# Counting with one input: VectorE's threshold counts as a tensor_scalar with an accumulator, and the memory keys transposed after the tenth folding turn

## The chip, the cores and the metric

The kernel runs on one core of a Trainium2 chip. The core has TensorE (PE; weight loads are shown as PEld), VectorE (DVE), ScalarE (ACT), GpSimd (POOL) and SyncE (SP), which issues the DMAs. The metric is the time of one launch on the device, in microseconds (us); lower is better. Three runs before the change took 2820.49, 2822.4 and 2825.87 us; the median is 2822.4.

## The reference

The input x is 8 batches of 512 tokens of 256 numbers, in fp32. Two layers follow. The first adds to x an attention and an FFN, both of the layer-normed x; the second adds a long convolution with a gated FFN, and an int4 linear layer with a low-rank side branch. The attention is what the change touches (cut to what matters):

```python
# H = 16 heads of DH = 64, NUM_MEM = 64 learned memory keys in front, TOPK = 64
q, k, v = split(x @ Wq.T), split(x @ Wk.T), split(x @ Wv.T)
k, v = concat([mem_k, k]), concat([mem_v, v])
dots = einsum('bhid,bhjd->bhij', q, k) * DH ** -0.5
dots = einsum('bhij,hk->bkij', dots, pre_proj)          # mixes the heads
dots = where(causal, -max, dots)
kth = top_k(dots, TOPK)[0][..., -1:]                     # the 64th largest of each row
dots = where(dots < kth, -max, dots)
attn = einsum('bhij,hk->bkij', softmax(dots), post_proj) # mixes the heads again
out = (attn @ v) @ Wout.T + bout
```

The FFN of the first layer quantises activations and weights to FP4 in blocks of 16 numbers; the int4 layer rounds its weight matrix with one scale for the whole matrix.

## The kernel before

**Stages.** A preparation (0 to about 120 us) loads and transposes weights, quantises the FFN's weights, rounds the int4 matrix and folds Wq, Wk and pre_proj into one matrix per mixed head (`mg`, and `mgm` for the memory keys). Then comes the attention (to about 2200 us), then the rest of both layers (to the end). Beside the attention's last groups, the FFN of batch 0 already runs.

**The folding.** It goes in `NJ` = 20 turns `j`, each over 16 dimensions: turns 0 to 15 over those of x, turns 16 to 19 over the 64 memory keys. A turn multiplies `bd` (block-diagonal copies of Wk, and of the transposed memory keys for the last four turns) with `wq` into a bank `pa`, copies it to `both` (ScalarE in even turns, VectorE in odd ones), multiplies with `kr` (pre_proj spread out) into a bank `pm`, which ScalarE copies to `mg` or `mgm` and squares; VectorE adds the squares up (`sqp`). The sums give, for each mixed head, the size of its scores, from which `first_guesses` computes a first threshold for every row. The memory keys `mk` need eight transposes on TensorE and two copies on VectorE into `bd`; before the change these stand ahead of the first turn in the program.

**The attention.** Queries are taken in 64 groups (8 batches of 8 groups) of 64 tokens; a group has 8 blocks of 8 tokens. One block's scores lie with 16 heads x 8 tokens on the 128 partitions and the keys along the free axis: 64 memory keys and the causal keys, from 72 to 576 numbers in fp32. The 64th largest score of each of the 128 rows is found by counting. `search` makes six rounds (`ROUNDS`); in each, every block counts how many of its scores reach the current threshold `cur`. `na` says how many of a group's 8 blocks ScalarE counts: 8 in the first three rounds, 0 in the last three, which VectorE counts; the first two groups (`EDGE`) and the last four (`LAST`) split some rounds with `na` = 4. ScalarE counts with Sign and an accumulator (L1079), VectorE with a compare and an accumulator (L1083). Both give `raw`; `base[na] - raw` is twice the distance of the count from its aim, whichever engine counted: the table `base` holds one number per block for each `na`. Between rounds `narrow` (L1099 to L1132) makes a secant step to the next threshold: on POOL after ScalarE's rounds, on VectorE after its own. After the sixth round the distance goes to `foff` (L1209).

Then VectorE takes the eight scores just under or over the threshold (`under`, L1140, and MAX8, L1143) and picks the 64th (`pick`, L1148 to L1152); ScalarE computes the exponentials `e` (L1158); VectorE drops what lies below the 64th and sums up (`keep_top`, L1167), and takes the reciprocal `rden` (L1252). POOL multiplies it into the second head mix (`mixd`, L1260), with which TensorE turns the scores (`ps_at`, L1303) and multiplies by the values (`ps_y`, L1327). Ahead of a group, TensorE makes the mixed queries (`ps_mi`, L997) and the scores (`ps_sc`, L1037), which ScalarE copies out (`tk`, L1008, and `ring`, L1043).

**The order.** A planner (`Plan`) with a fixed cost for each operation and due times writes the order of every engine's queue ahead of time. The preparation goes through `Straight`, which records each call, derives dependencies from the tiles that it reads and writes (as ranges of partitions and columns, so two interleaved patterns in one tile count as overlapping), and orders by the longest chain behind an operation; `r.late` shifts an operation's due time. DMAs are planned with the rest and issued by SP in that order. Records made through `Straight` all carry the line L235, so their tiles tell them apart. The pools of the attention take the memory of the preparation, so that the attention's first gather (`rows`, L955) waits for the preparation's last store.

The lines that a sentence can't say are VectorE's count and the two places where it is used:

```python
nc.vector.scalar_tensor_tensor(
    junk, src, thr, two.to_broadcast([P, src.shape[-1]]), ALU.is_ge,
    ALU.mult, accum_out=raw[:, b : b + 1],
)
...
eng.tensor_tensor(cur[:, 1], base[na][:, own], w["raw"], ALU.subtract)
nc.vector.tensor_tensor(w["off"], base[na][:, g * GB : (g + 1) * GB], w["raw"], ALU.subtract)
```

`two` is one column of -2.0 per partition, read again for every key as the second input, so `raw` is -2 times the count.

Of the kernel before, what the change touches and what calls it, by code (L numbers as in the profile page):

```python
# [11 lines left out]
ALU = mybir.AluOpType  # L12
# [7 lines left out]
H, DH = 16, 64  # L20
HC = H * DH // P
MEM = 64
# [4 lines left out]
GB = 8  # L27
# [15 lines left out]
AIM = LOW + 3.5  # L43
# [553 lines left out]
def block_kernel(ctx: ExitStack, tc: tile.TileContext, a: dict, out: bass.AP):  # L597
    nc = tc.nc
# [47 lines left out]
    with ExitStack() as c0:  # L646
# [14 lines left out]

        io8 = keep.tile([P, 8], F32, name="io8")
        base = {}
        for na in sorted({na for na, _ in ROUNDS + EDGE + LAST}):
            base[na] = keep.tile([P, NB], F32, name=f"base{na}")
        minus = keep.tile([P, GB], F32, name="minus")
        good = keep.tile([P, NB], F32, name="good")
# [9 lines left out]
        with tc.tile_pool(name="prep", bufs=1) as prep, tc.tile_pool(name="prep_ps", bufs=1, space=PSUM) as pps:  # L677
# [5 lines left out]
            def bank(kind):  # L683
                own = {"a": banks[:2], "m": banks[2:5], "t": banks[5:]}[kind]
                used[kind] = used.get(kind, -1) + 1
                return own[used[kind] % len(own)]
# [34 lines left out]
            for j0 in range(0, 16, 8):  # L721
                for t in range(2):
                    for i in range(2):
# [3 lines left out]
                            bd[rows, half, j0 : j0 + 8, t, :],  # L727
                            wkm[rows, half, j0 * 16 : (j0 + 8) * 16].rearrange("p c (j i) -> p c j i", i=16),
                        )
            r.late = 30.0  # L730
            ps = bank("t")
            for c in range(HC):
                r.tensor.transpose(
                    ps[:, c * MEM : (c + 1) * MEM],
                    mk[:, 2 * c : 2 * c + 2, :].rearrange("m h d -> m (h d)"),
                    ident[:MEM, :MEM],
                )
            for t in range(2):
                rows = slice(t * DH, (t + 1) * DH)
                r.vector.tensor_copy(bd[rows, :, 16:, t, :], ps[rows].rearrange("p (c j i) -> p c j i", c=HC, i=16))  # L740
            r.late = 0.0

            row16 = prep.tile([P, 16], F32, name="row16")
            r.vector.tensor_reduce(row16, ident.rearrange("p (k i) -> p i k", i=16), AX.X, ALU.add)
# [9 lines left out]
            for j in range(NJ):  # L754
                pa = bank("a")
                for i in range(2):
                    for u in range(4):
                        c = 4 * i + u
                        r.tensor.matmul(
                            pa[u * 32 : (u + 1) * 32, i * D : (i + 1) * D], bd[:, c, j].rearrange("p t i -> p (t i)"),  # L760
                            wq[:, c, :], start=True, stop=True,
                        )
                ab = both[j % 3]
                (r.scalar.copy, r.vector.tensor_copy)[j % 2](ab, pa)
                pm = bank("m")
                for e in range(DC):
                    for i in range(2):
                        r.tensor.matmul(
                            pm[:, e * D : (e + 1) * D], ab[:, i * D + e * P : i * D + (e + 1) * P],
                            kr[:, i].rearrange("p k i -> p (k i)"), start=(i == 0), stop=(i == 1),  # L770
                        )
                dst = mg[:, :, :, j * 16 : (j + 1) * 16] if j < 16 else mgm[:, :, :, (j - 16) * 16 : (j - 15) * 16]
                r.scalar.copy(dst, pm.rearrange("p (e k i) -> p e k i", e=DC, i=16))
                r.scalar.activation(junk[j % 2], pm, AF.Square)
                r.vector.tensor_reduce(sqp[:, j], junk[j % 2].rearrange("p (q i) -> p q i", i=16), AX.X, ALU.add)
# [293 lines left out]
        def block(s, g, b):  # L1069
            return s[:, b, : keys(g * GB + b)]  # L1070

        def count(g, s, cur, raw, b, on_act):


            src = block(s, g, b)
            thr = cur[:, 0, b : b + 1]
            junk = wp.tile([P, WD[-1]], I8, name=f"junk{int(on_act)}")[:, : src.shape[-1]]
            if on_act:
                nc.scalar.activation(  # L1079
                    junk, src, AF.Sign, bias=thr, scale=-1.0, accum_out=raw[:, b : b + 1]  # L1080
                )
            else:
                nc.vector.scalar_tensor_tensor(  # L1083
                    junk, src, thr, two.to_broadcast([P, src.shape[-1]]), ALU.is_ge,
                    ALU.mult, accum_out=raw[:, b : b + 1],
                )

        def narrow(g, w, k, na, on_pool):

# [6 lines left out]
                return st.tile([P] + shape, F32, name=name, bufs=4)  # L1096

            cur, prev = w["cur"], w.get("prev")
            eng.tensor_tensor(cur[:, 1], base[na][:, own], w["raw"], ALU.subtract)  # L1099
            w["prev"] = cur  # L1100
            w["cur"] = nxt = st.tile([P, 2, GB], F32, name="cur", bufs=14)
            by = new("by", [GB])
# [78 lines left out]
        def search(pl, g, s, w, deps, rounds):  # L1181
# [6 lines left out]
            for k, (na, on_pool) in enumerate(rounds):  # L1188
# [4 lines left out]
                tail = pl.add("none", 0.0, open_, [tail])  # L1193
                for b in range(GB):
                    def one_count(b=b, na=na):
                        count(g, s, w["cur"], w["raw"], b, b < na)

                    n = keys(g * GB + b)
                    counts.append(
                        pl.add("ACT", 0.28 + 0.00083 * n, one_count, deps + [tail]) if b < na else  # L1200
                        pl.add("DVE", 0.17 + 0.00105 * n, one_count, deps + [tail])
                    )

                def step(k=k, na=na, on_pool=on_pool):
                    if k < len(ROUNDS) - 1:
                        narrow(g, w, k, na, on_pool)
                    else:
                        w["off"] = st.tile([P, GB], F32, name="foff", bufs=4)
                        nc.vector.tensor_tensor(w["off"], base[na][:, g * GB : (g + 1) * GB], w["raw"], ALU.subtract)  # L1209

                last = k == len(ROUNDS) - 1
                tail = pl.add(
# [659 lines left out]
```

## Time and profile before

| | |
|---|---|
| runs | 2820.49, 2822.4, 2825.87 us (median 2822.4) |
| the profiled execution | 2827.49 us, span 2825.8 us, granted clock 0.951 |
| busy in the span | PE 2531.3, PEld 1963.4, DVE 2440.1, ACT 2031.5, POOL 1191.1 us |
| VectorE's counts, L1083 | 1512 instructions, 578 ns in the mean, and 1512 reads of the accumulator, 81 ns |
| ScalarE's counts, L1079 | 1560 instructions, 562 ns in the mean, and 1560 reads of the accumulator, 196 ns |

A profile is one execution on the chip. A line of a group reads: source line, engine, operation, output tile <- input tiles, shapes, how many; then the busy time and the mean of one in ns; then how long the engine was idle just before them and what ended most of that idle time. In a timeline the first two numbers are the start and the duration in us; "x8" at the end says that eight instructions in a row were merged, and brackets give the idle time before and what ended it. The unit called PEq, POOLq or SPq is the sequencer of that engine.

### The profile page before, as it was taken

What the parts mean: (1) busy time and instruction counts of PE and PEld (TensorE: products, weight loads), DVE (VectorE), ACT (ScalarE), POOL (GpSimd) and SP (SyncE); (2) the same over time, 40 slices, a digit from 0 to 9 for tenths busy, and PEclk for the clock granted to TensorE, in tenths of its full rate; (3) what the DMA queues carried; (4) which work ended last, traced back from release to release, by engine and by line L of the source; (5) the groups of instructions that cost most, each with busy time, mean ns of one, the idle gap of its engine ahead of it and who ended that gap; (6) DMA issues with size and microseconds to landing.
All of it is one profiled execution on the core that took longest, in us unless ns stands there. A gap on an engine that the chain in (4) does not pass through costs nothing. (4 is left out here: it accounts for less than half of the span.)

```text
span 2825.8 us, 57533 instructions
## 1 busy us (share of the span) xinstructions
PE 2531.3 (90%) x19064; PEld 1963.4 (69%) x19064; DVE 2440.1 (86%) x7978; ACT 2031.5 (72%) x5876; POOL 1191.1 (42%) x2215
## 2 busy tenths in 40 slices
PE   5999999999999999999999999999976578999997
PEld 3676877787687778777776786777665455666664
DVE  6678989999999999999999999999989869877762
ACT  3478887888888888888888887887888445544442
POOL 3204544445443544444354444445345344444320
PEclk9999999999999999999999999999988789999998
DMA  4300010100000000001000010000010031000000
GB/s 135 147 26 16 25 30 17 28 19 19 21 26 19 26 21 26 21 19 28 19 27 10 28 30 15 21 21 28 25 42 7 6 109 30 23 16 15 8 8 15
DMA packets 114872, 82.71 MB, mean 29 GB/s; under 512 B 79339, under 2 KB 108806, under 8 KB 113798
## 3 DMA queue, kind: packets, MB, share of 16 engines
q1 hardware_dynamic: 114566, 78.95, 9.2%
q8 instruction: 153, 2.51, 0.4%
q14 instruction: 153, 1.25, 0.1%
HBM read 44.04 MB, written 35.39 MB: 28 GB/s over the span
## 5 line engine op out<-in xcount | busy, mean ns | idle before, releaser
L1079 ACT ACTIVATE junk<-ring,cur 128x312 int8<-128x312 f32 (+26 forms) x1560 | 864.9, 562 | 22.9 <-POOL cur L1185 13.6
L1083 DVE SCALAR_TENSOR_TENSOR junk<-ring,cur,two 128x72 int8<-128x72 f32 (+9 forms) x1512 | 826.9, 578 | 10.4 <-POOL cur L1132 7.8
L1037 PE MATMUL ps_sc<-xnT,tk 128*128 128x8 f32 (+38 forms) x2048 | 540.6, 411 | 52.0 <-ACT ring L1043 51.3
L997 PE MATMUL ps_mi<-rows,mg 128*128 128x128 f32 x4096 | 518.2, 283 | 39.1 <-ACT scr L974 22.5
L997 PEld LDWEIGHTS ps_mi<-rows,mg 128*128 128x128 f32 x4096 | 495.1, 197 | 66.5 <-ACT scr L974 27.8
L1037 PEld LDWEIGHTS ps_sc<-xnT,tk 128*128 128x128 f32 x2048 | 351.6, 201 | 204.7 <-issue 76.1
L1303 PE MATMUL ps_at<-mixd,ring 128*128 128x128 f32 x2560 | 338.9, 284 | 24.1 <-POOL mixd L1260 21.9
L1099 POOL TENSOR_TENSOR cur<-base,raw 128x8 f32<-128x8 f32 x186 | 55.9, 300 | 704.4 <-ACT junk L1079 656.6
L1303 PEld LDWEIGHTS ps_at<-mixd,ring 128*128 128x128 f32 x2560 | 311.8, 195 | 49.8 <-POOL mixd L1260 28.2
L1167 DVE SCALAR_TENSOR_TENSOR ring<-ring,kth,e 128x520 f32<-128x520 f32 (+56 forms) x512 | 276.5, 562 | 75.3 <-ACT e L1158 72.2
L1079 ACT ACTIVATION_READ_ACCUMULATOR junk<-ring,cur 128x1 f32 x1560 | 305.4, 196 | 0.0
L1140 DVE SCALAR_TENSOR_TENSOR y<-ring,cur 128x520 f32<-128x520 f32 (+56 forms) x512 | 295.5, 577 | 3.4
L1143 DVE MAX8 top<-y 128x8 f32<-128x520 f32 (+56 forms) x512 | 255.4, 499 | 17.6
L1043 ACT COPY ring<-ps_sc 128x456 f32<-128x456 f32 (+56 forms) x512 | 186.7, 377 | 112.4 <-PE ps_sc L1037 107.9
L1309 ACT COPY at<-ps_at 128x512 f32<-128x512 f32 x320 | 185.7, 581 | 107.7 <-PE ps_at L1303 105.6
L1327 PE MATMUL ps_y<-at,v 128*64 128x64 f32 (+1 forms) x6144 | 221.5, 225 | 18.7 <-ACT at L1291 12.0
L1158 ACT ACTIVATE e<-ring 128x520 f32<-128x520 f32 (+56 forms) x512 | 229.1, 471 | 12.1 <-DVE ring L1167 11.5
L1327 PEld LDWEIGHTS ps_y<-at,v 128*64 128x64 f32 (+1 forms) x6144 | 197.4, 138 | 55.9 <-ACT at L1291 19.6
L1122 POOL TENSOR_TENSOR by<-gap,minus 128x8 f32<-128x8 f32 x124 | 219.6, 1771 | 9.7
L1008 ACT COPY tk<-ps_mi 128x256 f32<-128x256 f32 x512 | 170.9, 378 | 65.3 <-PE ps_mi L997 64.9
L1260 POOL TENSOR_TENSOR mixd<-mix,rden 128x512 f32<-128x512 f32 x128 | 145.1, 1152 | 141.3 <-DVE rden L1252 95.1
L235 PE MATMUL ps_gu<-mg,ring 128*128 128x352 f32 x448 | 148.4, 476 | 16.5 <-DVE hid L235 10.3
(319 smaller groups left out, 4030.1 us busy)
## 6 DMA issues: line engine op xcount, KB each, us to landing
msd<-scr SPq DMA_DIRECT2D x32, 512.0 KB
ring<-msd SPq DMA_DIRECT2D x512, 32.0 KB
scr<-in_L_attn_x_dram SPq DMA_DIRECT2D x10, 512.0 KB
mg_d<-mg SPq DMA_DIRECT2D x1, 4096.0 KB
att<-o SPq DMA_DIRECT2D x64, 64.0 KB
ring<-in_L_attn_x_dram SPq DMA_DIRECT2D x8, 512.0 KB
ring<-att SPq DMA_DIRECT2D x8, 512.0 KB
out_dram<-ring SPq DMA_DIRECT2D x8, 512.0 KB
```

What stands on the lines that cost most here:

```text
L997: nc.tensor.matmul(ps[:, j * P : (j + 1) * P], mg[:, e, k + j, e2 * P : (e2 + 1) * P], toks(e), start=(e == 0), stop=(e == DC - 1),)
L1037: nc.tensor.matmul(ps[:, :ntok], q["tk"][side_of(g)][e][:, b].rearrange("p k i -> p (k i)"), o["xnT"][:, e, :ntok], start=(e == 0), stop=( ...
L1043: nc.scalar.copy(s[:, b, MEM : MEM + ntok], q.pop(("ps", b))[:, :ntok])
L1079: nc.scalar.activation(junk, src, AF.Sign, bias=thr, scale=-1.0, accum_out=raw[:, b : b + 1])
L1083: nc.vector.scalar_tensor_tensor(junk, src, thr, two.to_broadcast([P, src.shape[-1]]), ALU.is_ge, ALU.mult, accum_out=raw[:, b : b + 1],)
L1122: eng.tensor_tensor(by, gap[:, 1], minus, ALU.pow)
L1140: nc.vector.scalar_tensor_tensor(y, src, cur[:, 0, b : b + 1], src, ALU.is_ge, ALU.subtract, reverse1=True)
L1143: nc.vector.max(out=top[:, b, :], in_=y)
L1158: nc.scalar.activation(e, src, AF.Exp, scale=1.0 / SMALL)
L1167: nc.vector.scalar_tensor_tensor(src, src, kth[:, b : b + 1], e, ALU.is_ge, ALU.mult, accum_out=den[:, b : b + 1])
L1303: nc.tensor.matmul(pt[:n, b * P : (b + 1) * P], s[:, 4 * j + b, col : col + n], w["mix"][j][:, b, :], start=True, stop=True,)
L1327: nc.tensor.matmul(w["py"][j * DH : (j + 1) * DH, q * GR : (q + 1) * GR], vs[c][:n, k * DH : (k + 1) * DH], ats[c][:n, k, :], start=(c == ...
```

## The change

Two things change.

First, where VectorE counts all 8 blocks of a round (`na` = 0), the count becomes a `tensor_scalar`: it compares the scores with the threshold, adds 0.0, and its accumulator adds the result up. It has one input tensor; the column `two` is not read. `raw` is then the count itself, and a new function `excess` turns it into twice the distance from the aim with a multiply and an add, in place of the subtraction from `base`. The table for `na` = 0 goes. Rounds with `na` = 4 or 8 stay as they are.

Second, the transposes and copies of the memory keys move from ahead of the folding turns into turn 9, behind its copy to `both`. In the planner, the last of the transposes also gets that copy as something to come after. The due time's shift of 30 goes.

```diff
-        for na in sorted({na for na, _ in ROUNDS + EDGE + LAST}):
+        for na in sorted({na for na, _ in ROUNDS + EDGE + LAST} - {0}):
...
-            r.late = 30.0
-            ps = bank("t")
-            for c in range(HC):
-                r.tensor.transpose(
-                    ps[:, c * MEM : (c + 1) * MEM],
-                    mk[:, 2 * c : 2 * c + 2, :].rearrange("m h d -> m (h d)"),
-                    ident[:MEM, :MEM],
-                )
-            for t in range(2):
-                rows = slice(t * DH, (t + 1) * DH)
-                r.vector.tensor_copy(bd[rows, :, 16:, t, :], ps[rows].rearrange("p (c j i) -> p c j i", c=HC, i=16))
-            r.late = 0.0
...
-                (r.scalar.copy, r.vector.tensor_copy)[j % 2](ab, pa)
+                op = (r.scalar.copy, r.vector.tensor_copy)[j % 2](ab, pa)
+                if j == 9:
+
+                    ps = bank("t")
+                    for c in range(HC):
+                        mk_op = r.tensor.transpose(
+                            ps[:, c * MEM : (c + 1) * MEM],
+                            mk[:, 2 * c : 2 * c + 2, :].rearrange("m h d -> m (h d)"),
+                            ident[:MEM, :MEM],
+                        )
+                    mk_op.after.append(op)
+                    for t in range(2):
+                        rows = slice(t * DH, (t + 1) * DH)
+                        r.vector.tensor_copy(
+                            bd[rows, :, 16:, t, :], ps[rows].rearrange("p (c j i) -> p c j i", c=HC, i=16)
+                        )
...
-        def count(g, s, cur, raw, b, on_act):
+        def count(g, s, cur, raw, b, na):
+            on_act = b < na
...
+            elif na == 0:
+                nc.vector.tensor_scalar(junk, src, thr, 0.0, ALU.is_ge, ALU.add, accum_out=raw[:, b : b + 1])
             else:
                 nc.vector.scalar_tensor_tensor(
...
+        def excess(eng, to, g, raw, na):
+
+            if na == 0:
+                eng.tensor_scalar(to, raw, 2.0, -2.0 * AIM, ALU.mult, ALU.add)
+            else:
+                eng.tensor_tensor(to, base[na][:, g * GB : (g + 1) * GB], raw, ALU.subtract)
...
-            eng.tensor_tensor(cur[:, 1], base[na][:, own], w["raw"], ALU.subtract)
+            excess(eng, cur[:, 1], g, w["raw"], na)
...
-                        count(g, s, w["cur"], w["raw"], b, b < na)
+                        count(g, s, w["cur"], w["raw"], b, na)
...
-                        nc.vector.tensor_tensor(w["off"], base[na][:, g * GB : (g + 1) * GB], w["raw"], ALU.subtract)
+                        excess(nc.vector, w["off"], g, w["raw"], na)
```

## The prediction

> **What bounds the kernel now.** I read the page first (engines, costliest groups), then the busy time by stretch, then which waits end the idle time of TensorE and VectorE in the middle of the run, then the timelines of single counts, of the start and of the three engines around 1017 us. The page:
>
> ```profile
> PE 2531.3 (90%) x19064; PEld 1963.4 (69%) x19064; DVE 2440.1 (86%) x7978; ACT 2031.5 (72%) x5876; POOL 1191.1 (42%) x2215
> ...
> L1079 ACT ACTIVATE junk<-ring,cur 128x312 int8<-128x312 f32 (+26 forms) x1560 | 864.9, 562 | 22.9 <-POOL cur L1185 13.6
> L1083 DVE SCALAR_TENSOR_TENSOR junk<-ring,cur,two 128x72 int8<-128x72 f32 (+9 forms) x1512 | 826.9, 578 | 10.4 <-POOL cur L1132 7.8
> ```
>
> The line that changes, L1083, is a third of VectorE's time. The stretches show that the 2060 us of attention (140 to 2200) decide:
>
> ```profile
> 0.00:140.00 140.00, 102.58 (x735) 72.70 (x736) 93.92 (x235) 58.45 (x121) 42.96 (x156) 0.96 0.42 142
> 140.00:2200.00 2060.00, 1901.38 (x16163) 1538.12 (x16161) 1896.38 (x6896) 1700.58 (x5274) 909.27 (x1907) 0.96 0.08 23
> ```
>
> The columns are stretch, then PE, PEld, DVE, ACT, POOL busy, clock, DMA share, GB/s. PE is idle for 158.6 us and DVE for 163.6 us there: two engines nearly full, in queues of a fixed order. What ends PE's idle time (300 to 2000 us):
>
> ```profile
> L1037 PE MATMUL ps_sc<-xnT,tk 128*128 128x264 f32 (+61 forms) x1728 | 450.7, 407 | 40.1 <-ACT ring L1043 39.5
> L997 PE MATMUL ps_mi<-rows,mg 128*128 128x128 f32 x3440 | 439.1, 284 | 37.2 <-ACT scr L974 22.5 <-ACT tk L1008 14.7
> L1303 PE MATMUL ps_at<-mixd,ring 128*128 128x128 f32 x2140 | 280.4, 283 | 14.3 <-POOL mixd L1260 13.8 <-ACT at L1309 0.5
> ```
>
> PE waits mostly for ScalarE's evictions, and only 13.8 us for mixd, the one wait behind which VectorE stands (POOL's mixd waits for DVE's rden, 67.1 us in the waits of that window). VectorE's own wait is for ScalarE's exponentials:
>
> ```profile
> L1083 DVE SCALAR_TENSOR_TENSOR junk<-ring,cur,two 128x192 int8<-128x192 f32 (+57 forms) x1287 | 698.7, 573 | 7.3 <-POOL cur L1132 5.3
> ...
> L1167 DVE SCALAR_TENSOR_TENSOR ring<-ring,kth,e 128x200 f32<-128x200 f32 (+61 forms) x431 | 229.3, 554 | 62.0 <-ACT e L1158 59.1
> ```
>
> So VectorE is full, but a microsecond saved on it is not a microsecond of the end.
>
> **The counts.** 1440 of the 1512 counts (all with na = 0) become a tensor_scalar with an accumulator; 72 stay. On all engines the order of the attention's instructions is the same before and after, so only durations change. One count, alone and beside POOL's mixd (first VectorE, then POOL):
>
> ```profile
> 1016.24 0.65 DVE L1083 SCALAR_TENSOR_TENSOR junk<-ring,cur,two 128x416 int8<-128x416 f32 x1
> 1016.81 0.09 DVE L1083 DVE_READ_ACCUMULATOR junk<-ring,cur,two 128x1 f32 x1
> ...
> 1017.46 1.45 DVE L1083 SCALAR_TENSOR_TENSOR junk<-ring,cur,two 128x432 int8<-128x432 f32 x1
> ...
> 1018.83 1.44 DVE L1083 SCALAR_TENSOR_TENSOR junk<-ring,cur,two 128x440 int8<-128x440 f32 x1
> ```
>
> ```profile
> 1017.21 2.59 POOL L1260 TENSOR_TENSOR mixd<-mix,rden 128x512 f32<-128x512 f32 x2 [3.44 <-PE ps_at L1283]
> ```
>
> Undisturbed, the forms 128x408 (634 ns) and 128x416 (641 ns) give n/0.96 + 208 ns. The blocks run from 72 to 576 keys, 324 in the mean, so an undisturbed mean count is 338 + 208 = 546 ns. The page has 578: 32 ns, times 1440 46 us, is time in which a count stands still while POOL reads. The trace has no tensor_scalar with an accumulator. Its neighbours: L302, a tensor_scalar with pointer scalars, 128x256, steps in 1.38/4 = 345 ns = 133 + 212 where two elements pass per cycle; the 128x512 tensor_scalar of the start takes 0.41 us against 0.68 for the two-input form; the accumulator's read (81 ns) stays. Bounds for 1440 counts: half of n/0.96 goes, 169 ns each, 243 us of VectorE less; or one more fixed part, the 65 ns by which pointer forms (208) exceed immediate ones (143), 94 us more. I take one element per cycle and the same fixed part, the nearest rows being the same compare with an accumulator, and the 46 us gone: VectorE's other one-input instruction of this stage, MAX8, takes 0.24 us at 1252.50 beside a mixd as without one, where the two-input L1140 just before it (128x72; a 128x88 alone takes 0.30) took 1.08.
>
> [...]
>
> What of the 46 us reaches the end? The attention's waits that POOL or VectorE end on the other engines, 300 to 2000 us: PE for mixd 13.8, ACT's counts for cur 13.6 + 2.1, VectorE's for cur 5.3, together 35 us; 2060/1700 of that is 42. POOL's short steps are stretched too (L1099 0.64 us at 1001.17 beside a count of 1001.14, its 8-element steps at 1013 us 0.20), so these waits shrink from both sides; on the other hand the next two-input instruction (L1140, L1167) may meet the mixd that a count met. I take 40% of them, 16 us, for the attention, bounds 0 (ScalarE's evictions own the path) and 46 (all of it).
>
> **The excess.** 180 TENSOR_TENSORs (116 at L1099, 64 at L1209, 164 to 219 ns) become tensor_scalars on the same engine in the same place; a short tensor_scalar takes 170 ns (L288, 126.67 us). Between -9 and +5 us of VectorE, none of the end; the waits behind it are those above.
>
> **The memory keys.** Eight transposes and two copies move from the head of PE's and VectorE's queues behind the tenth of twenty folding turns, and the planner, with another longest chain, reorders the start: on SP, Wk, Wq and the two pre_proj loads go ahead of the four w_gate/w_up loads, x, Wv, mk and Wout; VectorE's bd and kr copies ahead of the first weights' quantisation; on PE the first ten turns ahead of the transposes of x, Wv and Wout. Before:
>
> ```profile
> 16.28 1.08 PE L235 MATMUL pps<-ident,mk 64*128 64x64 f32 x8 [16.28 <-DMA mk<-in_L_attn_mem_k_dram]
> ...
> 36.96 3.22 PE L235 MATMUL pps<-ring,bd 128*32 128x256 f32 x32
> ...
> 116.12 0.43 PE L235 MATMUL pps<-sq,ones 128*128 128x64 f32 x2 [0.37 <-DVE sq L235]
> ```
>
> ```profile
> 121.48 0.40 POOL L955 COPY rows<-xnT 128x256 f32<-128x256 f32 x1 [11.65 <-DMA w_d<-w1s]
> ```
>
> Attention starts at 121.48, after the store of w1s. PE's preparation is 83 us of products (73 after 36.96, 10 before). Wk and Wq, 2 MB at the 250 to 370 GB/s of the first 15 us, with bd and kr, let the first turn start near 11 us. Fed without a stop PE would end at 94, 22 us earlier. It isn't: x's transposes wait for VectorE's x rows, which stand behind the second w_gate/w_up pair, issued some 3 us later than before (five small loads now precede it; it landed at 29.8 and 32.6), a stop near 33 to 38 us. The int4 kernel's load overwrites Wv, whose transposes now follow eight turns (to about 45), so its maximum comes near 49 instead of 38.14, and POOL's all-reduce, which held POOL until 49.89, 11 us behind that maximum, holds it to about 60. The second pair's last products thus come 8 to 10 us later, the third pair and w_down follow, each bound to the one before by its two buffers; before, w_down's last steps (102 to 105 us on POOL) waited for PE, not for their loads (VectorE idle until 94.6). I carry 103 for them and some 9 us of products behind: 112 instead of 116.5. That is -4 us, bounds -22 and +10. All engines wait for the store, so it moves the end one for one.
>
> **Sum.** -16 -4 = -20 us on the profiled execution's 2827.5 (span 2825.8 and 1.7 around it), which lies 5.1 over the median of 2822.4; so 2802 for the median. Bounds: -46 -22 and 0 +10. 0.2% (5.6 us) is what a measurement can tell from nothing.
>
> **Rivals.**
> 1. Two elements per cycle. For: the plain form's 0.41 us. Against: no accumulating row shows it. VectorE drops from 1896 to about 1653 us of 2060, no mixd wait is left, and ScalarE's counts and evictions (1701 busy, 77 us of PE's idle time) own the path: 42 us of waits all gone, with the start's 4: about 2776. [...]
> 2. Hidden anyway. For: PE's longest waits end with ACT, and PE has 1901 of 2060 us. Counts shrink, VectorE waits longer for e (59.1 us now). Only the start is left: 2819.
> 3. The accumulating form costs more (slower). The extra part of 65 ns on 1440 counts is 94 us, less 46: 48 more on an engine with 163.6 idle, of which a third waits for e. From about 35 ns per count on it outweighs contention and start; half of the 48 at the end, less 4: 2842. Against: two-input accumulating rows already carry pointer and accumulator.
> 4. The start gets longer. VectorE's order puts turn copies behind loads; +10 with the counts hidden: 2832.
>
> **Chances.** Forecast 0.53 (its own range 2785 to 2817), rival 1 0.13, rival 2 0.15, rival 3 0.13, rival 4 0.06. Faster: 0.53 + 0.13 = 0.66; same 0.15; slower 0.19. The range runs from rival 1 (2776) to rival 4 (2832), leaving out rival 3 and a little more.
>
> **What would show it.** Counts whose undisturbed 128x416 stays near 641 ns, with a mean near 546 and none at 1.4 us beside mixd; POOL's L1099 nearer 200 ns; PE's mixd wait under 13.8 us. The first bd product near 11 us and rows' start near 117. A 128x416 near 430 ns is rival 1, above 670 rival 3; unchanged stage times with longer VectorE waits for e, rival 2; a rows start after 121.5, rival 4. Wrong altogether: other engines slowed by the counts' new use of memory.

## The result, and the profile after

The changed kernel takes 2790.35 us (median of four runs, 2786.24 to 2791.80); the kernel before took 2824.14 us beside it. The ratio is 0.9876 (95% interval 0.9856 to 0.9897), 35 us. That is faster, inside the predicted range and 12 us below the forecast of 2802. The profiled execution took 2786.24 us, with a span of 2784.5 us and a granted clock of 0.955.

The page of the changed kernel: the busy times, then the costliest groups that touch the change (busy us, mean ns of one | idle time just before and what ended it).

```profile
PE 2510.5 (90%) x19064; PEld 1945.8 (70%) x19064; DVE 2387.1 (86%) x7978; ACT 2030.5 (73%) x5876; POOL 1060.7 (38%) x2214
...
L1083 ACT ACTIVATE junk<-ring,cur 128x312 int8<-128x312 f32 (+26 forms) x1560 | 864.8, 562 | 10.8 <-POOL cur L1145 5.8
L1087 DVE TENSOR_SCALAR_CACHE_REDUCE junk<-ring,cur 128x344 int8<-128x344 f32 (+30 forms) x1440 | 733.0, 541 | 4.8 <-POOL cur L1145 3.1
```

The new counts are the L1087 group, under a name that the trace before did not have. One takes 541 ns in the mean against a forecast of 546; a 128x416 one takes 636 ns, so one element passes in 1/0.96 ns, the prediction's cycle (416/0.96 + 203; a line through the medians of its 64 lengths rises by 1.044 ns an element, that of the old form by 1.045). VectorE is 53 us less busy. POOL, whose work hardly changed, is 130 us less busy, which is the line to be surprised at.

Beside POOL's mixd a count now runs on as if it were alone:

```profile
930.66 0.78 DVE L1087 TENSOR_SCALAR_CACHE_REDUCE junk<-ring,cur 128x552 int8<-128x552 f32 x1
931.37 0.08 DVE L1087 DVE_READ_ACCUMULATOR junk<-ring,cur 128x1 f32 x1
931.37 0.79 DVE L1087 TENSOR_SCALAR_CACHE_REDUCE junk<-ring,cur 128x560 int8<-128x560 f32 x1
```

The 0.78 us of the first, under a mixd that runs from 930.74 to 932.78, is the undisturbed 552/0.96 + 205 ns. Of the 1440 new counts none took over 20 ns more than n/0.96 + 204 ns; of the 1512 old ones 129 took over 20 ns more than n/0.96 + 208 ns, 47 us in all.

The stretches of the changed kernel (columns: PE, PEld, DVE, ACT, POOL busy, clock, DMA share, GB/s):

```profile
0.00:140.00 140.00, 112.17 (x794) 80.13 (x795) 102.14 (x265) 63.06 (x131) 43.75 (x156) 0.93 0.44 147
140.00:2200.00 2060.00, 1894.73 (x16294) 1531.92 (x16293) 1878.40 (x6989) 1713.90 (x5303) 794.91 (x1921) 0.97 0.08 22
```

In the same 2060 us TensorE now does 16294 products instead of 16163 and is busy for 7 us less; the clock reads 0.97 instead of 0.96. POOL's 909 us became 795.

What ends the idle time of TensorE and VectorE, 300 to 2000 us:

```profile
L1040 PE MATMUL ps_sc<-xnT,tk 128*128 128x280 f32 (+62 forms) x1750 | 458.2, 407 | 41.2 <-ACT ring L1046 40.7
L1000 PE MATMUL ps_mi<-rows,mg 128*128 128x128 f32 x3472 | 439.0, 282 | 39.6 <-ACT scr L977 26.3 <-ACT tk L1011 13.3
L1316 PE MATMUL ps_at<-mixd,ring 128*128 128x128 f32 x2184 | 281.6, 280 | 2.1 <-POOL mixd L1273 1.6 <-ACT at L1322 0.5
...
L1180 DVE SCALAR_TENSOR_TENSOR ring<-ring,kth,e 128x240 f32<-128x240 f32 (+62 forms) x435 | 230.5, 552 | 83.4 <-ACT e L1171 80.5
```

TensorE's three waits for ScalarE stayed near what they were (40.7, 26.3 and 13.3 us, together 80.3 against 76.7), its wait for mixd fell from 13.8 to 1.6 us, and VectorE waits longer for ScalarE's exponentials (80.5 instead of 59.1): 21 us of what VectorE saved it now waits there.

Milestones of the two profiled executions, in us:

| | before | after | difference |
|---|---|---|---|
| first `rows` copy (start of attention) | 121.5 | 111.5 | -10.0 |
| first group's `rden` | 236.4 | 223.4 | -13.0 |
| 10th group's `rden` | 513.6 | 490.3 | -23.3 |
| 31st | 1177.9 | 1149.8 | -28.1 |
| last (64th) | 2250.4 | 2206.1 | -44.3 |
| end of the span | 2825.8 | 2784.5 | -41.3 |

So the start gave about 10 us, and the attention, from first to last `rden`, 31: 2014.0 became 1982.7 us. The first group's way to its `rden` gave 3 more, and the part behind the last `rden` lost 3. (The two profiled executions lie 41 us apart, the medians 34.)

### The profile page after: what moved, and what is told of

Read it like the earlier page. It is cut to its first block, busy times and chain, and to the rows that moved or that the text cites. A ratio compares the mean times of both kernels' runs of the same rounds, so it can differ in the third digit from the quotient of the medians.

```text
span 2784.5 us, 57532 instructions
## 1 busy us (share of the span) xinstructions
PE 2510.5 (90%) x19064; PEld 1945.8 (70%) x19064; DVE 2387.1 (86%) x7978; ACT 2030.5 (73%) x5876; POOL 1060.7 (38%) x2214
## 5 line engine op out<-in xcount | busy, mean ns | idle before, releaser
L1087 DVE TENSOR_SCALAR_CACHE_REDUCE junk<-ring,cur 128x344 int8<-128x344 f32 (+30 forms) x1440 | 733.0, 541 | 4.8 <-POOL cur L1145 3.1
L1040 PE MATMUL ps_sc<-xnT,tk 128*128 128x8 f32 (+38 forms) x2048 | 535.0, 406 | 52.0 <-ACT ring L1046 51.4
L1000 PE MATMUL ps_mi<-rows,mg 128*128 128x128 f32 x4096 | 514.0, 281 | 41.6 <-ACT scr L977 26.3
L1040 PEld LDWEIGHTS ps_sc<-xnT,tk 128*128 128x128 f32 x2048 | 345.4, 197 | 205.6 <-issue 77.0
L1316 PE MATMUL ps_at<-mixd,ring 128*128 128x128 f32 x2560 | 332.9, 281 | 11.9 <-POOL mixd L1273 9.7
L1099 POOL TENSOR_TENSOR cur<-base,raw 128x8 f32<-128x8 f32 x186 | 48.7, 262 | 734.4 <-ACT junk L1083 677.9
L1171 ACT ACTIVATE e<-ring 128x520 f32<-128x520 f32 (+56 forms) x512 | 229.0, 471 | 11.6 <-DVE ring L1180 11.2
L1135 POOL TENSOR_TENSOR by<-gap,minus 128x8 f32<-128x8 f32 x124 | 207.8, 1676 | 9.7
L1273 POOL TENSOR_TENSOR mixd<-mix,rden 128x512 f32<-128x512 f32 x128 | 131.7, 1049 | 155.8 <-DVE rden L1265 124.2
```

Source lines behind the costliest of these rows:

```text
L1000: nc.tensor.matmul(ps[:, j * P : (j + 1) * P], mg[:, e, k + j, e2 * P : (e2 + 1) * P], toks(e), start=(e == 0), stop=(e == DC - 1),)
L1040: nc.tensor.matmul(ps[:, :ntok], q["tk"][side_of(g)][e][:, b].rearrange("p k i -> p (k i)"), o["xnT"][:, e, :ntok], start=(e == 0), stop=( ...
L1087: nc.vector.tensor_scalar(junk, src, thr, 0.0, ALU.is_ge, ALU.add, accum_out=raw[:, b : b + 1])
L1135: eng.tensor_tensor(by, gap[:, 1], minus, ALU.pow)
L1171: nc.scalar.activation(e, src, AF.Exp, scale=1.0 / SMALL)
L1316: nc.tensor.matmul(pt[:n, b * P : (b + 1) * P], s[:, 4 * j + b, col : col + n], w["mix"][j][:, b, :], start=True, stop=True,)
```

## Where the attention gained: experiments

**1. Counts alone.** The new kernel with the memory keys back ahead of the turns:

```diff
+            r.late = 30.0
+            ps = bank("t")
+            for c in range(HC):
+                r.tensor.transpose(ps[:, c * MEM : (c + 1) * MEM], ...)
...
-                if j == 9:
-                    ps = bank("t")
...
```

> The new counts and the new excess, with the memory keys back in their old place ahead of the turns. Theory A (the two parts add up; the counts own most of the gain, because the 46 us that VectorE stood still beside POOL are gone): 23 to 27 us under the kernel before, rows' start near 121.5 us as before, and the attention's groups gaining about 0.5 us each. Rival B (the gain came with the new start, which also shifts the attention's work against the loads): 10 us or less under the kernel before. Rival C (the parts help each other): the two parts alone fall short of 33.8 us by more than 5.

Measured: 2795.08 us, ratio 0.9890 (0.9872 to 0.9907), 31 us under the kernel before, more than the 23 to 27 of theory A. From first to last `rden` it takes 1984.0 us, as the full change does. The start of `rows` came at 118.7 us, 2.8 earlier than before, though nothing of the order of the start is the change's; the single profiled executions scatter by that much. The counts own the attention's gain, and rival B falls.

**2. Memory keys alone.** The kernel before with the second part only (the diff above, the other way round, on the old counts).

> Only the memory keys moved behind the tenth turn; counts and excess as before. Theory A: 10 us under the kernel before, all of it ahead of the attention (rows start near 111.5 us instead of 121.5), and the attention as long as before, with counts still stretched beside POOL's mixd. Rival B: 20 to 30 us under. The forecast on record had 4 us for this part, from preparation products that end near 112 us; the trace of the changed kernel has them at 107.5.

Measured: 2812.68 us, ratio 0.9949 (0.9936 to 0.9963), by which it is 14 us less (10 to 18). `rows` start at 113.8 us, the last `rden` lies 9.1 us earlier, and the attention takes 2012.9 us, as before. The two parts alone give 31 + 14 = 45 us against 35 together, 10 more, where the intervals of 5, 4 and 6 us allow some 9 if their errors are independent. In the traces the parts simply add up: the attention gains 30.0 + 1.1 us against 31.3 together, and `rows` come 2.8 + 7.7 us earlier against 10.0. So rival C falls, and why the ratios give more than the traces stays open.

**3 to 5. VectorE's time given back.** The changed kernel with a write of 8, 80 or 160 elements behind every second count:

```diff
                 nc.vector.tensor_scalar(junk, src, thr, 0.0, ALU.is_ge, ALU.add, accum_out=raw[:, b : b + 1])
+                if b % 2:
+                    nc.vector.memset(idle, 0.0)
```

> The changed kernel with 720 short VectorE writes (an 8-element memset behind every second one-input count, an estimated 65 ns each, 47 us in all), which add nothing to the result: VectorE gets back about the time that the old counts lost beside POOL, without touching POOL or memory contention. Theory A (what shortened the attention is VectorE's time): it loses 15 to 25 us on the changed kernel and comes out about 10 to 17 us under the kernel before. Rival D (what shortened it is that POOL's steps and its mixd are no longer slowed, VectorE's own time being covered by its waits for ScalarE's exponentials): it loses 5 us or less, 28 us or more under the kernel before.

Measured: 2787.30 us, ratio 0.9865 (0.9849 to 0.9880). That is rival D's number, but the run does not decide it. The trace shows 720 writes of 65 ns, and yet the step from count to count did not grow (1.84 us over two counts and one block of `under` and MAX8, with and without the write): the short write runs beside the accumulator's read or the start of the next instruction (one starts at 1002.01 us, beside a read that started at 1001.97 and lasts 0.08 us and an `under` that started at 1001.99). So the size was raised.

> The changed kernel with an 80-element VectorE write behind every second one-input count (720 of them, nothing of the result depends on them). The 8-element writes of the run before took no time: the step from one count to the next stayed 1.52 to 1.54 us per block, because they ran in the shadow of the accumulator's read. At 2.19 us for 2560 elements (the start's write of bd, 0.83 ns each) 72 elements more are an estimated 60 ns each, 43 us of VectorE in all, about what the old counts lost. Theory A (VectorE's own time shortened the attention): 12 to 25 us slower than the changed kernel, 0.992 to 0.997 of the kernel before. Rival D (POOL's freed steps did): at most 5 us slower, 0.986 to 0.9895 of the kernel before.

Measured: 2786.12 us, ratio 0.9851 (0.9835 to 0.9868); attention 1983.1 us. These writes were mostly hidden too: VectorE's busy time from 140 to 2190 us rose by 10 us, not by 43.

> The same with 160 elements: an estimated 126 ns each, 91 us of VectorE, twice what the old counts lost. Theory A: 30 to 50 us slower than the changed kernel, at or above the kernel before (0.998 to 1.006). Rival D: at most 15 us slower than the changed kernel, since VectorE then has about as little idle time as the kernel before had: 0.988 to 0.993.

Measured: 2791.53 us, ratio 0.9872 (0.9856 to 0.9889); attention 1979.9 us. Here the time was given back. The stretch 140 to 2190 us, of this kernel:

```profile
140.00:2190.00 2050.00, 1890.42 (x16282) 1530.84 (x16280) 1914.77 (x7692) 1711.20 (x5299) 784.86 (x1918) 0.97 0.08 22
```

and of the kernel before:

```profile
140.00:2190.00 2050.00, 1894.79 (x16115) 1532.98 (x16113) 1886.59 (x6871) 1696.28 (x5268) 907.67 (x1906) 0.96 0.08 23
```

VectorE is busy for 1914.8 us, 46 more than in the changed kernel (1868.6) and 28 more than in the kernel before, and nothing is lost. Most of it came out of what VectorE waits for the exponentials (45.4 us in place of 80.5). Theory A, that the 46 us of VectorE's own standing still were the gain, is refuted; and it was the sum's own theory.

**6. POOL's time given back, spread.** The changed kernel with a 392-element write in all 186 narrowing steps on POOL:

```diff
             excess(eng, cur[:, 1], g, w["raw"], na)
+            if on_pool:
+                nc.gpsimd.memset(idle, 0.0)
```

> The changed kernel with a 392-element POOL write in each of POOL's 186 narrowing steps, behind the excess (nothing of the result depends on it). The same shape takes 424 ns in the clearing of the ring, so 79 us of POOL come back, 0.42 us in each step of the search; the steps had become some 0.46 us shorter (POOL's lines of the steps sum to 85 us less than before). VectorE's counts stay free of contention. Theory A: at most 5 us slower than the changed kernel (0.986 to 0.9895 of the kernel before). Rival D: 12 to 25 us slower (0.992 to 0.997).

Measured: 2789.82 us, ratio 0.9867 (0.9851 to 0.9884); attention 1985.8 us, 3 more. POOL got 79 us of writes (186 of 425 ns; its busy time from 140 to 2190 us rose by 56), and the run did not lose them. The ratio is the one that theory A forecast, which run 5 refutes, and rival D's 12 to 25 us did not come: POOL's sum is not it either. But the trace shows more than the time: the steps grew by about 0.25 us in most places and not at all in one, the 24th of each 24 (4.79 us with and without, the first time apart), behind which TensorE used to wait.

**What the traces show at that place.** The waits of TensorE over a microsecond, listed by their place, repeat every eight groups (252.3 to 252.6 us before from 705 us on, 248.9 to 249.6 after). Before, one in each period is for mixd, always 1.87 us: at 450.46, 705.14, 957.48, 1209.99, 1462.55 and 1715.17 us. After, these are gone. POOL's timeline ahead of the wait at 957.48, kernel before (the step whose last instruction is at 957.64, then mixd):

```profile
950.57 0.42 POOL L1099 TENSOR_TENSOR cur<-base,raw 128x8 f32<-128x8 f32 x1 [5.03 <-DVE cur L1132]
951.06 0.38 POOL L1109 TENSOR_TENSOR same<-cur 128x8 f32<-128x8 f32 x1
951.53 0.64 POOL L1112 TENSOR_SCALAR same<-same 128x8 f32<-128x8 f32 x1
...
952.73 0.73 POOL L1119 TENSOR_TENSOR step<-cur 128x16 f32<-128x16 f32 x1
...
954.01 2.06 POOL L1122 TENSOR_TENSOR by<-gap,minus 128x8 f32<-128x8 f32 x1
956.15 0.68 POOL L1125 TENSOR_TENSOR by<-by,gap 128x8 f32<-128x8 f32 x1
956.90 0.65 POOL L1131 TENSOR_TENSOR by<-by,cur 128x8 f32<-128x8 f32 x1
957.64 0.66 POOL L1132 TENSOR_TENSOR cur<-cur,by 128x8 f32<-128x8 f32 x1
958.26 2.03 POOL L1260 TENSOR_TENSOR mixd<-mix,rden 128x512 f32<-128x512 f32 x2
```

VectorE in the same stretch, kernel before:

```profile
954.48 0.20 DVE L1252 RECIPROCAL rden<-den 128x8 f32<-128x8 f32 x1
...
955.97 0.80 DVE L1083 SCALAR_TENSOR_TENSOR junk<-ring,cur,two 128x560 int8<-128x560 f32 x1
956.69 0.81 DVE L1083 SCALAR_TENSOR_TENSOR junk<-ring,cur,two 128x568 int8<-128x568 f32 x1
957.42 0.81 DVE L1083 SCALAR_TENSOR_TENSOR junk<-ring,cur,two 128x576 int8<-128x576 f32 x1
```

and TensorE:

```profile
959.35 1.82 PE L1303 MATMUL ps_at<-mixd,ring 128*128 128x128 f32 x13 [1.87 <-POOL mixd L1260]
```

`rden` is there at 954.68, and mixd starts 3.6 us later, because POOL is still in another group's narrowing step. The step's last three instructions, of 8 elements each, start 0.74 us apart, at the rate at which VectorE finishes its 0.8-us counts: each count holds one of them off. The same place in the changed kernel:

```profile
928.27 1.66 POOL L1135 TENSOR_TENSOR by<-gap,minus 128x8 f32<-128x8 f32 x1
930.02 0.20 POOL L1138 TENSOR_TENSOR by<-by,gap 128x8 f32<-128x8 f32 x1
930.30 0.20 POOL L1144 TENSOR_TENSOR by<-by,cur 128x8 f32<-128x8 f32 x1
930.58 0.20 POOL L1145 TENSOR_TENSOR cur<-cur,by 128x8 f32<-128x8 f32 x1
930.74 2.04 POOL L1273 TENSOR_TENSOR mixd<-mix,rden 128x512 f32<-128x512 f32 x2
```

The three take 0.20 us each and start 0.28 us apart; the whole step takes 4.79 us instead of 7.73, `rden` comes at 930.09 and mixd starts 0.65 us behind it. From this a new theory (E below): what counts is the direction opposite to the one that the sum priced, VectorE stretching POOL, and it counts at one place in eight groups.

**7. That step alone made longer.** The changed kernel with seven POOL writes in every 24th narrowing step:

```diff
             excess(eng, cur[:, 1], g, w["raw"], na)
+            if on_pool:
+                turns.append(k)
+                for _ in range(7 if len(turns) % 24 == 0 else 0):
+                    nc.gpsimd.memset(idle, 0.0)
```

> The changed kernel with seven 392-element POOL writes (424 ns each, 2.97 us together; nothing of the result depends on them) in every 24th narrowing step of POOL alone, seven times in all. That is the step which ran 7.73 us before and runs 4.79 us after, with mixd queued behind it. Theory E (the attention was shortened at this one place in each eight groups: VectorE's counts no longer stretch this step, so mixd no longer comes late to TensorE): TensorE waits some 1.9 us for mixd again in each period, half-clock slots come back behind that wait, and the run is 12 to 22 us slower than the changed kernel, 0.992 to 0.996 of the kernel before. Rival F (the gain is spread over all steps): only the 21 us of POOL are added, one place in 24, and 3 us or less are lost.

Measured: 2802.16 us, ratio 0.9913 (0.9897 to 0.9930); attention 1999.5 us, 16.8 more than the changed kernel. TensorE's wait, 300 to 2000 us, this kernel:

```profile
L1322 PE MATMUL ps_at<-mixd,ring 128*128 128x128 f32 x2176 | 281.8, 281 | 12.6 <-POOL mixd L1279 12.2 <-ACT at L1328 0.5
```

The step takes 7.54 us and the wait is back (1.67 to 1.76 us in each period). 21 us of POOL in the right place cost what 79 us spread out did not.

**8. 56 new counts in the old kernel.** The kernel before, with the one-input form only where counts run beside that step:

```diff
+            elif one:
+                nc.vector.tensor_scalar(junk, src, thr, 0.0, ALU.is_ge, ALU.add, accum_out=raw[:, b : b + 1])
...
-                        count(g, s, w["cur"], w["raw"], b, b < na)
+                        count(g, s, w["cur"], w["raw"], b, b < na, g == 7 and k == 4 and na == 0)
```

> The kernel before with the one-input form in 56 of its 1440 counts only: those of the largest group's fifth round, which run beside that POOL step. The start stays as before. Theory E: 12 to 22 us faster than the kernel before (0.992 to 0.996), the step near 4.8 us and the 1.87 us wait for mixd gone. Rival F: 56 of 1440 counts bring 56/1440 of about 31 us, 1 us (0.999 to 1.001).

Measured: 2800.60 us, ratio 0.9906 (0.9890 to 0.9923), 27 us under the kernel before with a start that has not moved (`rows` at 121.3); attention 1991.5 us. The wait of this kernel:

```profile
L1308 PE MATMUL ps_at<-mixd,ring 128*128 128x128 f32 x2201 | 285.6, 281 | 3.1 <-POOL mixd L1265 2.6 <-ACT at L1314 0.5
```

The step takes 4.79 us. One count in 26 brings 22.5 of the attention's 31 us.

**9. The same 56 counts undone in the changed kernel.**

```diff
-            elif na == 0:
+            elif na == 0 and not two_in:
...
-                        count(g, s, w["cur"], w["raw"], b, na)
+                        count(g, s, w["cur"], w["raw"], b, na, g == 7 and k == 4)
```

> The changed kernel with the old two-input form back in 56 of its 1440 counts only, those of the largest group's fifth round, which the run on 56 new counts showed to be worth 25 us in the kernel before. Theory E: the POOL step beside them grows from 4.79 to about 7.7 us, TensorE waits some 1.9 us for mixd in each period, and the run loses 12 to 25 us on the changed kernel (0.992 to 0.9965 of the kernel before). Rival F: 1 us or less (0.987 to 0.989).

Measured: 2804.11 us, ratio 0.9919 (0.9905 to 0.9932); attention 1999.9 us, 17.2 more than the changed kernel. The wait of this kernel:

```profile
L1319 PE MATMUL ps_at<-mixd,ring 128*128 128x128 f32 x2176 | 281.8, 281 | 13.3 <-POOL mixd L1276 12.9 <-ACT at L1325 0.5
```

Runs 7, 8 and 9 agree: this one step owns 17 to 22.5 us of the attention's 31. VectorE's own time has no part in it: the 56 two-input counts of run 9 took less than 0.1 us in all over n/0.96 + 208 ns, and the run lost 17 us with them. In ratio they lie a little outside what theory E expected (0.9913, 0.9906 and 0.9919 against 0.992 and more), and rival F's ranges lie outside all three intervals. The rest, some 9 to 14 us, was not taken apart; about half of it lies in the first ten groups (4.4 of 8.8 us in run 8), whose waits and clock changed too.

**The clock's part.** A wait of 1.87 us in each of six periods is 11 us, and the runs move by 17 to 22. The trace's record of the granted clock has the remainder in it. It knows two values here, whole and half, in slots of 3.41 us (but for the one cut off at the end, each of the 88 stretches that it lists before and of the 74 after is a whole number of 3.413 us). Half-clock time from first to last `rden`, beside the waits and the stretch:

| kernel | TensorE's wait for mixd, 300 to 2000 us | time at half clock | first to last `rden` |
|---|---|---|---|
| before | 13.8 | 180 | 2014.0 |
| changed | 1.6 | 146 | 1982.7 |
| 1, counts alone | 1.6 | 146 | 1984.0 |
| 2, memory keys alone | 13.5 | 176 | 2012.9 |
| 5, 160-element writes | 2.0 | 143 | 1979.9 |
| 7, step made longer | 12.2 | 160 | 1999.5 |
| 8, 56 counts new | 2.6 | 143 | 1991.5 |
| 9, 56 counts old | 12.9 | 164 | 1999.9 |

A 128x128 product of `ps_at` starts 112 ns behind the one before it at whole clock and 213 ns at half (medians of the kernel before), so 34 us less of it are up to 17 us of TensorE. That fits: from first to last `rden` both kernels do 15898 products, and TensorE's idle time there fell by 14.6 us (172.8 to 158.2; the wait for mixd alone by 12.2) and its busy time by 16.7. It does not fit everywhere: in run 8 idle and busy time fell by 11.2 and 11.3 us, where 37 us less at half clock would allow 18, and runs 3 and 6, with 140 us at half clock, took 1984.4 and 1985.8 us. Two such slots of the kernel before, each with the wait ahead of it:

```profile
1044.24:1047.85 3.61, 0.00 (x1) 0.00 (x0) 3.48 (x13) 3.61 (x11) 1.26 (x4) 0.82 0.00 0
1046.50:1053.40 6.90, 5.55 (x19) 4.52 (x20) 6.70 (x29) 4.56 (x17) 5.91 (x12) 0.51 0.24 44
450.46:452.33 1.87, 0.00 (x1) 0.00 (x0) 1.78 (x7) 0.65 (x2) 1.79 (x4) 1.00 0.02 4
452.60:456.00 3.40, 3.40 (x18) 3.40 (x18) 3.13 (x14) 0.66 (x2) 2.98 (x9) 0.50 0.09 19
```

and one of the changed kernel:

```profile
1017.47:1021.08 3.61, 0.00 (x1) 0.00 (x0) 3.20 (x11) 3.61 (x11) 1.23 (x4) 1.00 0.00 0
1022.00:1025.40 3.40, 3.40 (x13) 3.02 (x14) 3.26 (x18) 2.13 (x9) 3.01 (x7) 0.50 0.18 43
```

TensorE stands still in the first stretch of each pair (0.00 busy) and runs at half clock (0.51, 0.50) from within the wait or right behind it. The mixd wait at 450.46 had such a slot right behind it; the later ones did not. Behind the same 3.61-us wait for ScalarE the kernel before lost two slots and the changed one lost one. The slot at 452.6 us stands behind a wait of only 1.87 us, about half a slot. What sets a slot to half, and why the same wait cost two slots in one kernel and one in the other, no run here separates.

The length of the periods shows the price in another way. Between the 3.6-us waits for `ring` that come once in each, the periods settle: 252.6 us in the mean of the last three in the kernel before and in runs 2, 7 and 9, where TensorE waits for mixd once in each, and 249.1 to 249.3 in the changed kernel and in runs 1, 3 to 6, 8 and 11, where it does not. 74 slots of 3.413 us are 252.6 us and 73 are 249.2. So a period gave up one whole slot for a wait of 1.87 us, and five or six such periods make 17 to 20 us. This also weakens the reading of runs 3 to 6: if a period keeps to whole slots, it can swallow extra work until the next slot is due. No run here varies that, so why the periods fit whole slots, and how much runs 3 to 6 owe to it, stays open. Runs 7 to 9 do not lean on them.

**10. Relief for ScalarE.** Two of ScalarE's eight counts of the third round go to VectorE, in the changed kernel.

```diff
-ROUNDS = ((GB, True), (GB, True), (GB, True), (0, False), (0, False), (0, False))
+ROUNDS = ((GB, True), (GB, True), (GB - 2, True), (0, False), (0, False), (0, False))
```

> The changed kernel with two of the eight ScalarE counts of the third round moved to VectorE, where 91 us more cost nothing in the run with 160-element writes: an estimated 128 x 0.75 = 96 us off ScalarE's queue, on whose evictions TensorE waits 80 us between 300 and 2000 us, and 128 x 0.58 = 74 us onto VectorE, in the two-input form. If ScalarE's queue bounds TensorE's waits: 10 to 30 us faster than the changed kernel. If the planner's new order or the two-input counts beside POOL cost more than that: 0 to 30 us slower.

Measured: 2847.85 us, ratio 1.0071 (1.0051 to 1.0090), about 55 us slower than the changed kernel and outside both ranges. (The 91 us of the expectation is the estimate; by the trace VectorE's busy time rose by 46 in run 5.) The waits of this kernel, 300 to 2000 us:

```profile
L1000 PE MATMUL ps_mi<-rows,mg 128*128 128x128 f32 x3424 | 456.4, 292 | 63.7 <-ACT tk L1011 35.5 <-ACT scr L977 28.1
L1040 PE MATMUL ps_sc<-xnT,tk 128*128 128x280 f32 (+29 forms) x1696 | 432.4, 400 | 11.1 <-ACT ring L1046 10.9
L1316 PE MATMUL ps_at<-mixd,ring 128*128 128x128 f32 x2112 | 285.4, 289 | 25.4 <-POOL mixd L1273 25.4
```

ScalarE is 86 us less busy (1624 of 2050 us against 1711), and yet TensorE waits for it about as long as before: 30 us less for `ring` and 22 more for `tk`, and in all 84 us instead of 86. Its wait for mixd grew from 1.6 to 25.4 us, that for `rows` from 0.5 to 10.9, and the time at half clock from 146 to 192. The planner wrote another order, in which these come late. The run changed the order and the two-input counts together, so it does not tell their parts.

## Where the start gained

The start came out right in mechanism and too small in size. Kernel after, TensorE and VectorE:

```profile
7.97 3.80 PE L235 MATMUL pps<-ring,bd 128*32 128x256 f32 x32 [7.97 <-DVE bd L235]
...
36.71 3.64 PE L235 MATMUL pps<-ring,bd 128*32 128x256 f32 x32 [8.04 <-DVE both L235]
```

```profile
31.55 0.69 DVE L235 TENSOR_REDUCE w_amax<-w_v 128x32 f32<-128x512 f32 x1 [6.13 <-DMA w_v<-in_L_ffn_w_up_dram]
```

The first turn runs at 7.97 us instead of 36.96. TensorE then stops for 8 us, since the eighth turn's copy to `both` stands in VectorE's queue behind a maximum that waits for the third row block of w_gate and w_up (the first of what the prediction calls the second pair). POOL's first instruction behind the all-reduce starts at 57.9 (forecast: about 60). From 62.6 to 98 us VectorE has no wait of a microsecond: the third pair's last POOL products end at 78 us, w_down's at 97.4, and the preparation's products at 107.0. The store of `w1s` is issued at 107.5 (116.5 before); `rows` start here:

```profile
111.52 0.40 POOL L958 COPY rows<-xnT 128x256 f32<-128x256 f32 x1 [14.04 <-DMA w_d<-w1s]
```

**11. The third load earlier.** To see whether VectorE's queue now sets the start, the load of that row block was put ahead of ten other loads on SP:

```diff
+            third = [op for n, op in r.loads if "w_gate" in n or "w_up" in n][4:6]
+            for n, op in r.loads:
+                if any(k in n for k in ("attn_Wg", "Wfg", "Wfu", "attn_bo", "ffn_bias", "L1_ffn_a", ...)):
+                    op.after += third
             pl.tails()
```

> The changed kernel with the load of the third w_gate/w_up pair ahead of ten other small loads on SP: after the change it was issued only at 27.18 us, behind loads that took SP from 21.4 to 27.1, landed at 31.5, and VectorE stood for 6.1 us in front of it with the turns' copies queued behind. If VectorE's queue is what the start now hangs on (no wait of over 0.7 us from 62.6 to 98 us): the load is issued near 21.5 us, rows start 3 to 6 us earlier, near 106 to 108, and the run is 3 to 6 us faster than the changed kernel. If the start hangs on the later loads or on the products: within 2 us of the changed kernel.

Measured: 2781.49 us, ratio 0.9841 (0.9827 to 0.9854), the fastest kernel of the study. Its load and its `rows`:

```profile
21.92 0.36 SPq L236 DMA_DIRECT2D w_v<-in_L_ffn_w_gate_dram  x1
22.32 0.44 SPq L236 DMA_DIRECT2D w_v<-in_L_ffn_w_up_dram  x1
```

```profile
107.12 0.40 POOL L964 COPY rows<-xnT 128x256 f32<-128x256 f32 x1 [15.54 <-DMA w_d<-w1s]
```

The load is issued 5.3 us earlier (21.92 instead of 27.18), VectorE stops for 2.7 us at the block behind it instead of 6.1, and `rows` start 4.4 us earlier. The medians differ by 9 us across two sets of runs, the traced start explains 4.4 of them, and the interval of the ratios does not separate the rest from scatter. That is what VectorE's queue as the start's limit had forecast (`rows` at 106 to 108); the ten loads that moved back in exchange cost nothing that shows.

## Why the prediction was right, and where it was wrong

- **Counts: one element per cycle and the same fixed part** held (541 ns against 546 in the mean; rival 1 needed 430 ns for 128x416 and rival 3 over 670, measured 636). That POOL no longer stretches them held for every one of 1440 (none over 20 ns more than n/0.96 + 204 ns). The pace of the plain `tensor_scalar` (0.41 us for 128x512 and 0.69 for 128x1024 in the kernel before, 0.53 ns an element) did not carry over to the form with an accumulator (0.74 us for 128x512 in the kernel after).
- **Attention: -16 forecast, about -31 measured.** This is the term that was mis-sized. It was made as 40% of the 42 us of waits behind VectorE and POOL, from 46 us of VectorE's lost time. The lost time itself was worth nothing that shows (run 5, and run 9, where 17 us go with less than 0.1 us of it). The other direction, which the working names in half a sentence ("POOL's short steps are stretched too"), carried it: POOL's 8-element steps waited a whole count each, one step in 24 stood ahead of mixd, and the 13.8 us of TensorE's wait went almost whole (12.2) instead of by 40%. On top came 34 us less at half clock, which the working did not have: it took a TensorE wait to cost its own length. That the total still fell inside the range is in part luck: the term was priced from VectorE's lost time, which proved worth nothing, and a direction named in passing and a clock that was not in the sum brought more than it had.
- **"A microsecond saved on VectorE is not a microsecond of the end"** held more strictly than it was meant.
- **The excess: nothing.** The L1097 groups took 191 and 190 ns against 219 and 164 before, about -1.6 us of VectorE in all: nothing.
- **The start: -4 forecast, -10 in the trace** (run 2 alone: 14 by the ratio, 10 to 18, and 9 in its trace). The first turn (11 forecast, 7.97), the stop (33 to 38 forecast, 28.7 to 36.7) and POOL's release by the all-reduce (60, 57.9) were near. The step that failed is "I carry 103" for w_down's last steps: they ended at 97.4, because the quantisation behind the all-reduce ran without a gap on VectorE, which the sum had slowed by two buffers and POOL. "Some 9 us of products behind" came to 9.6. The store behind them was issued 4.5 us ahead of the forecast's 112, and `rows`, forecast at 117, came 5.5 ahead.
- **Rival 2 (hidden anyway)** was half right: VectorE's time was hidden, behind the exponentials. It overlooked that the counts also set POOL's time. **Rival 4** (a longer start) did not happen.

The sum on record, -20, missed by 14 us of a measured 34 to 35, some 15 us in the attention and 6 in the start by the traces, whose two executions lie 7 us further apart than the medians.

## What to carry to other kernels

When two engines contend, price both directions, and price them at the places where a third engine waits: here 56 of 1440 instructions held more than half of the attention's gain, and giving VectorE back as much time as it had saved cost nothing. To find the place, list the bottleneck engine's longest waits by their time of day, look for the period, and read the other queues in the microseconds ahead of one of them. A filler instruction tests a theory only if the trace shows that it took time where it was put; of these five, the 8-element writes on VectorE hid, the 80-element ones mostly, and POOL's spread ones at the one place that mattered.

## What was not expected of the hardware

- POOL's 8-element instructions (0.20 us alone) took 0.65 to 0.68 us beside back-to-back two-input VectorE counts and advanced one per count. Of 372 such instructions 131 took over 0.3 us before, 33 after, 55 with the 56 old counts back.
- A VectorE write of 8 elements right behind an accumulating instruction (65 ns by its own record) added nothing to the step from count to count, and 720 of 80 elements (125 ns each, 90 us by their records) raised VectorE's busy time from 140 to 2190 us by 10 us only; with 160 elements (192 ns each, 138 us) it was 46.
- POOL's writes of 392 elements took 423 to 425 ns in the mean in the clearing of the ring before and after the change, where 49 and 50 of the 64 ran beside a count, and 425 in the fillers: a form that only writes was not stretched beside either form of count.
- A shorter wait of TensorE paid more than its length where the record shows half-clock slots: 12 us of waits went together with 34 us less at half clock.
